# A two-layer convolution network on one core: convolution blocks of one half of the images beside the MLP of the other half, tap matrices made by TensorE, and one pool of two PSUM slots

## The chip, the cores and the metric

The kernel runs on one core of one Trainium2 chip. A core has five engines that run their own queues: TensorE (PE, matmuls, whose weight loads the profile lists as PEld), VectorE (DVE), ScalarE (ACT), GpSimd (POOL) and SyncE (SP), which only issues transfers. Sixteen DMA engines move data between the chip's main memory (DRAM) and the core's SBUF; SP, ACT and POOL each have a queue that issues them. TensorE writes to PSUM, which has eight banks of 512 fp32 values in each of 128 partitions. The metric is device microseconds (us) of one execution.

## The reference

Input x has 32 images of 96 channels and 56 x 56 positions. Everything is fp32.

```python
# layer 0
h = depthwise_conv7x7(x) + conv_b                    # 96 channels, padding 3
h = (h - mean_c(h)) * rsqrt(var_c(h) + 1e-5) * ln_g + ln_b   # over the channels
h = gelu(h @ w1 + b1) @ w2 + b2                      # 96 -> 384 -> 96, at each position
x = h * layer_scale + x
# layer 1
x = silu(depthwise_conv5x5(x) + conv_b)              # padding 2
dts, Bs, Cs = split(x_proj_w @ x)                    # 6, 4 and 4 rows
delta = softplus(dt_w @ dts + dt_b)
P = exp(cumsum(max(delta * -exp(A_logs), log 1e-9))) # along the 3136 positions
hs = P * cumsum(delta * Bs * x / max(P, 1e-9))
y = sum_n(hs * Cs) + x * Ds
```

## The kernel before, in words

The work goes in four stages, one after the other. Between them the data lies in DRAM: conv1_d after the first convolution, block_d after the MLP, conv2_d after the second convolution; each exists twice, for the two halves g of 16 images.

*Setup* (lines 94 to 274). For each convolution the taps of a channel are a small matrix that is nonzero only near a diagonal (a band), because a block puts image rows on the partitions. taps() writes the taps with zeros around them (pad) to DRAM (taps_d), and weights() reads them back many times, shifted, into wide tiles w1s (7 x 7, 6.2 MB in 16 loads) and w2s_t (5 x 5, 4.6 MB in 4), all issued by ACT. The biases come the same way (bias_d). Small constants are loaded by POOL and worked up by VectorE and a few matmuls (L218, L225).

*First convolution* (lines 313 to 382): 48 blocks, two halves g times KB = 24 groups kb of four channels. load1 has SP issue 8 loads of x into one of four tiles, three blocks ahead. bands (L300) has POOL copy the block's matrices into the order that TensorE wants (we, 3 buffers, two blocks ahead). convolve (L287) is 64 matmuls, 8 taps on 8 parts of the array. ScalarE copies the result out of PSUM (ht, L352, 3 buffers) and squares it (sq, L354, 2 buffers); POOL issues ht to conv1_d (L356); VectorE adds ht and sq to sums (acc, four additions, L365 to L368). After a half's last block, four matmuls (pm, L373) sum over the channels and a short chain over ScalarE and VectorE gives rstd_t (L378 to L382). Each block takes 4 of the 8 PSUM banks.

*MLP* (lines 385 to 499): 28 groups n of image rows, each of two units u, 56 units in all. load2 loads h (12 transfers) and x (4), three buffers each. normed scales h by rstd, which a matmul spreads over the partitions (rb, L427, then VectorE, L433). expand(u, f), for three thirds f, makes 12 matmuls into ph (L442, one buffer of 4 banks) and a Gelu on ScalarE (g, L448, 6 buffers). second(u - 1, e), for three thirds e, makes 12 matmuls into po (L464, 3 banks) and a VectorE addition of bias and x into o (L469, 2 buffers); after a group POOL issues o to block_d (L480). The order that is written out is expand(u, 0), normed(u + 1), second(u - 1, 0), expand(u, 1), second(u - 1, 1), expand(u, 2), second(u - 1, 2). So each Gelu lies beside a part of second. The profile counts each fp32 matmul as two instructions.

*Second convolution* (lines 503 to 549): as the first, with 48 matmuls a block, loads from block_d (L517), a Silu out of PSUM (st, L541, 3 buffers) and four transfers to conv2_d on POOL (L545).

*Scan* (lines 553 to 791): loads xs, projects, and runs VectorE's scans and POOL's products. The change does not touch it.

Most instructions are pinned (`pin`), which keeps them in the order of the program on their engine; a scheduler places the others. Each queue is strictly in order: an instruction that waits holds up what stands behind it.

Of the kernel before, what the change touches and what calls it, by code (L numbers as in the profile page):

```python
# [8 lines left out]
F32 = mybir.dt.float32  # L9
# [6 lines left out]
B2, BI = 2, 16  # L16
# [14 lines left out]
PARTS = (2, 4, 6, 12)  # L31
LOW = 25
S1, S2 = K1 + 1, K2 + 1
WL1, WL2 = PR * S1 + 1, PR * S2 + 1
T1, T2 = 67, 67
# [8 lines left out]
NG = 3  # L44


@with_exitstack
def convnext_then_scan_kernel(
# [27 lines left out]
    taps1_d = dram.tile([C, T1 * S1 + 1], F32, name="taps1_d")  # L76
    taps2_d = dram.tile([C, T2 * S2 + 1], F32, name="taps2_d")
    bias1_d = dram.tile([C, WL1], F32, name="bias1_d")
    bias2_d = dram.tile([C, WL2], F32, name="bias2_d")
# [8 lines left out]

    def column(src, n, name):
        t = const.tile([n, 1], F32, name=name)  # L90
        nc.gpsimd.dma_start(t, src.rearrange("(p o) -> p o", o=1))
        return t

    c1b_t = const.tile([C, 1], F32, name="c1b_t")
    c2b_t = const.tile([C, 1], F32, name="c2b_t")
    wide = ExitStack()
    wpool = wide.enter_context(tc.tile_pool(name="wide", bufs=1))
    w2s_t = wpool.tile([128, KB, 2, WL2], F32, name="w2s_t")
    mid = ExitStack()
    rstd_t = mid.enter_context(tc.tile_pool(name="mid", bufs=1)).tile(  # L100
        [128, B2, 2, TOK], F32, name="rstd_t"
    )
    first = ExitStack()
    w1pool = first.enter_context(tc.tile_pool(name="w1p", bufs=1))
    w1s = [w1pool.tile([128, n, 2, WL1], F32, name=f"w1s_{i}") for i, n in enumerate(PARTS)]
    x1s = [w1pool.tile([128, 2, COLS], F32, name=f"x1_{i}") for i in range(4)]
    for t in x1s:
        nc.vector.memset(t, 1.0)
    prep_s = ExitStack()
    prep = prep_s.enter_context(tc.tile_pool(name="prep", bufs=1))  # L110
    prep_ps = prep_s.enter_context(tc.tile_pool(name="prep_ps", bufs=1, space=PSUM))

    def weights(t, taps_d, bias_d, k, n, k0, k1, zs):
        s, wl, row = k + 1, PR * (k + 1) + 1, n * (k + 1) + 1
        for i in range(Q):
            cp, h = divmod(i, 2)
            c0 = k0 * 4 + cp
            pin(nc.scalar.dma_start(
                t[i * PR : (i + 1) * PR].rearrange("p k j w -> p (k j) w"),
                at(taps_d, c0 * row + zs[h] * s, [[s, PR], [2 * row, 2 * (k1 - k0)], [1, wl]]),  # L120
            ))
            pin(nc.scalar.dma_start(
                t[i * PR + PR - 1 : (i + 1) * PR].rearrange("p k j w -> p (k j) w"),
                at(bias_d, c0 * wl, [[wl, 1], [2 * wl, 2 * (k1 - k0)], [1, wl]]),
            ))

    def taps(taps_d, bias_d, cw, cb, cb_t, k, z, n, down):
        s = k + 1
        kt = prep.tile([C, k * k], F32, name=f"kt{k}")
        nc.scalar.dma_start(kt, cw)  # L130
        nc.scalar.dma_start(cb_t, cb.rearrange("(p o) -> p o", o=1))
        pad = prep.tile([C, n * s + 1], F32, name=f"pad{k}")
        nc.vector.memset(pad, 0.0)
        for i in range(k):
            a = k - 1 - i if down else i
            for u in range(k):
                nc.vector.tensor_copy(
                    pad[:, 1 + (z + i) * s + u : 2 + (z + i) * s + u],
                    kt[:, a * k + k - 1 - u : a * k + k - u],
                )  # L140
        nc.scalar.dma_start(taps_d, pad)
        br = prep.tile([C, PR * s + 1], F32, name=f"br{k}")
        nc.vector.memset(br, 0.0)
        nc.vector.tensor_copy(
            br[:, : PR * s].rearrange("c (m u) -> c m u", u=s)[:, :, k - k // 2],
            cb_t.to_broadcast([C, PR]),
        )
        nc.scalar.dma_start(bias_d, br)

    taps(taps1_d, bias1_d, c1w, c1b, c1b_t, K1, Z1, T1, False)  # L150
    k0 = 0
    for t, n in zip(w1s, PARTS):
        weights(t, taps1_d, bias1_d, K1, T1, k0, k0 + n, (3, 0))
        k0 += n
    taps(taps2_d, bias2_d, c2w, c2b, c2b_t, K2, Z2, T2, True)
    weights(w2s_t, taps2_d, bias2_d, K2, T2, 0, KB, (0, 3))

    ident = const.tile([128, 128], F32, name="ident")
    make_identity(nc, ident)
    eps_t = const.tile([128, 1], F32, name="eps_t")  # L160
    nc.gpsimd.memset(eps_t, LN_EPS)
    lift_t = const.tile([128, 2], F32, name="lift_t")
    nc.gpsimd.memset(lift_t[:, 0:1], LIFT)
    nc.gpsimd.memset(lift_t[:, 1:2], -LIFT)

    g_t = column(ln_g, C, "g_t")
    lnb_t = column(ln_b, C, "lnb_t")
# [3 lines left out]
    nc.gpsimd.memset(bcw_t, 0.0)  # L171
    ls_b = const.tile([128, C], F32, name="ls_b")
    nc.gpsimd.dma_start(ls_b, ls.rearrange("(o n) -> o n", o=1).to_broadcast([128, C]))
    b1_t = const.tile([128, 3], F32, name="b1_t")
    nc.gpsimd.dma_start(b1_t, b1.rearrange("(f p) -> p f", p=128))
    w2_t = const.tile([128, 3, C], F32, name="w2_t")
    nc.gpsimd.dma_start(w2_t, w2.rearrange("(f p) c -> p f c", p=128))
    dt4_t = const.tile([128, C], F32, name="dt4_t")
    nc.gpsimd.memset(dt4_t, 0.0)
    b2_t = const.tile([128, 3], F32, name="b2_t")  # L180
    ls_t = const.tile([128, 3], F32, name="ls_t")
    for q in range(Q):
        rows = slice(q * PR, (q + 1) * PR)
        nc.gpsimd.dma_start(dt4_t[q * PR : q * PR + R], dtwT)
        nc.gpsimd.dma_start(dtb_t[rows], dtb.rearrange("(g p) -> p g", p=PR))
        nc.gpsimd.dma_start(ds_t[rows], ds.rearrange("(g p) -> p g", p=PR))
        for g in range(NG):
            nc.gpsimd.dma_start(
                bcw_t[rows, g, : R + 2 * N], xpT[g * PR : (g + 1) * PR, :]
            )  # L190
        nc.gpsimd.dma_start(b2_t[rows], b2.rearrange("(g p) -> p g", p=PR))
        nc.gpsimd.dma_start(ls_t[rows], ls.rearrange("(g p) -> p g", p=PR))
    a_t = const.tile([128, NG], F32, name="a_t")
    for g in range(NG):
        nc.gpsimd.dma_start(a_t[:, g : g + 1], at(alog, g * PR, [[1, PR], [C, N], [1, 1]]))

# [8 lines left out]
    pickr_t = const.tile([128, OCT, 128], F32, name="pickr_t")  # L205

    cen = prep.tile([C, C], F32, name="cen")
    nc.vector.tensor_scalar(cen, ident[:C, :C], -1.0 / C, None, ALU.add)
    cen4 = prep.tile([C, 3, Q, PR], F32, name="cen4")
    for q in range(Q):  # L210
        nc.vector.tensor_copy(cen4[:, :, q, :], cen.rearrange("c (g p) -> c g p", g=3))
    w1_t = prep.tile([C, F], F32, name="w1_t")
    nc.gpsimd.dma_start(w1_t, w1)
    w1g = prep.tile([C, F], F32, name="w1g")
    nc.vector.tensor_scalar(w1g, w1_t, g_t, None, ALU.mult)
    for g in range(3):
        ps = prep_ps.tile([128, 512], F32, name=f"ps_w1_{g}", tag="ps_w1", bufs=2)
        nc.tensor.matmul(  # L218
            ps[:, :F], lhsT=cen4[:, g].rearrange("c q p -> c (q p)"), rhs=w1g,
            start=True, stop=True,  # L220
        )
        nc.vector.tensor_copy(w1c_t[:, g, :], ps[:, :F])
    ps = prep_ps.tile([128, 512], F32, name="ps_b1")
    for f in range(3):
        nc.tensor.matmul(  # L225
            ps[:, f : f + 1], lhsT=w1_t[:, f * 128 : (f + 1) * 128], rhs=lnb_t,
            start=True, stop=True,
        )
    nc.vector.tensor_add(b1p_t, ps[:, :3], b1_t)
    for f in range(3):  # L230
        nc.vector.tensor_mul(w2_t[:, f, :], w2_t[:, f, :], ls_b)
    nc.vector.tensor_mul(b2p_t, b2_t, ls_t)

    nc.vector.memset(pick_t, 0.0)
    for q in range(Q):
        rows = slice(q * PR, (q + 1) * PR)
        for i in range(2):
            lo = q * PR + R + i * N
            nc.vector.tensor_copy(
                pick_t[rows, i, :].rearrange("p (c n) -> p c n", n=N),  # L240
                ident[rows, lo : lo + N].rearrange("p (o n) -> p o n", o=1).to_broadcast([PR, PR, N]),
            )
        nc.vector.tensor_copy(
            pickr_t[rows].rearrange("p o (s c) -> p o s c", s=Q),
            ident[rows, q * PR : q * PR + HH]
            .rearrange("p (o s u) -> p o s u", s=Q, u=1)
            .to_broadcast([PR, OCT, Q, PR]),
        )
    nc.vector.tensor_reduce(
        sel_t, ident.rearrange("p (c n) -> p c n", n=N), axis=mybir.AxisListType.X, op=ALU.add  # L250
    )
    nc.vector.tensor_reduce(
        jsum_t[:, :64], ident.rearrange("p (j s) -> p s j", j=2),
        axis=mybir.AxisListType.X, op=ALU.add,
    )
    nc.vector.tensor_scalar(jsum_t[:, :64], jsum_t[:, :64], 1.0 / C, None, ALU.mult)
    nc.vector.tensor_copy(jsum_t[:, 64:], jsum_t[:, :64])
    for q in range(Q):
        rows = slice(q * PR, (q + 1) * PR)
# [576 lines left out]
```

## Time and profile before

| | |
|---|---|
| three runs | 3502.12, 3511.12, 3516.37 us, median 3511.12 us |
| profiled execution | 3505.03 us, span 3503.2 us |
| mean granted TensorE clock | 0.855 |
| busy | PE 2966.6, DVE 2231.7, ACT 1708.8, POOL 1967.3 us |
| copies of the first convolution (L352) | first 100.24, twelfth 195.55, 24th 286.19, 25th 303.65, last 457.55 us |
| MLP matmuls | from 487.00 us, last po near 1360 us |
| Silus of the second convolution (L541) | first 1388.94, last 1690.31 us |

Times are microseconds from the first instruction. In the slices of the page each digit is the busy share of one fortieth of the span in tenths; PEclk is the clock granted to TensorE, DMA the mean busy share of the 16 DMA engines. A line of the timeline gives start, duration, engine, line, operation, output and inputs, shapes, and in brackets the engine's idle time before it and what ended that. A line of the waits gives who waited for whom: us in total, times, longest.

### The profile page before, as it was taken

To read this page: it belongs to the slowest core of one execution; us is meant where nothing else is said; L and a number is where in the kernel's file an instruction comes from. 1 tells how busy PE (TensorE), PEld (TensorE's weight loads), DVE (VectorE), ACT (ScalarE), POOL (GpSimd) and SP (SyncE) were. 2 spreads that over 40 slices of the span, in tenths; PEclk is the share of its full clock that TensorE was granted. 3 is DMA by queue.
4 is the path that set the end of the run, shared out by engine and by line. 5 is a ranking of instruction groups with operands and counts; after the bars stand their busy time and mean duration, and the time that the engine had idled before them with its cause. 6 is when DMAs were issued, how large, how long until landed. Compare 5 with 4: busy or idle time off the path is not lost.

```text
span 3503.2 us, 65347 instructions
## 1 busy us (share of the span) xinstructions
PE 2966.6 (85%) x27660; PEld 1071.5 (31%) x27660; DVE 2231.7 (64%) x1335; ACT 1708.8 (49%) x1729; POOL 1967.3 (56%) x1096
## 2 busy tenths in 40 slices
PE   2599969999999997888688888888888888888885
PEld 1455533333333332444222222222222222222221
DVE  2498942222222221000099999999999999999998
ACT  0344433333333332222276676666667667667664
POOL 3354500000000002555388888888888988888886
PEclk9799979999999998999767787777777788777776
DMA  8898964444444434999655665646555566554652
GB/s 129 198 250 237 262 165 137 134 127 136 143 143 134 136 112 100 276 280 282 170 149 141 161 167 156 160 129 161 162 153 158 139 161 174 158 161 123 172 156 75
DMA packets 372163, 575.46 MB, mean 164 GB/s; under 512 B 217216, under 2 KB 300848, under 8 KB 371872
## 3 DMA queue, kind: packets, MB, share of 16 engines
q1 hardware_dynamic: 332352, 432.29, 45.7%
q0 software_dynamic: 25424, 127.03, 12.0%
q10 hardware_dynamic: 14096, 11.97, 2.0%
q8 instruction: 218, 3.57, 0.4%
q14 instruction: 73, 0.60, 0.1%
HBM read 366.89 MB, written 204.22 MB: 163 GB/s over the span
## 4 chain that ended last, share of the span: by engine, by line
PE 53%; ACT 16%; DMA 14%; SPq 5%; issue 4%; POOL 4%; DVE 3%; POOLq 0%; ACTq 0%; DVEq 0%
PE ph L442 12%; PE po L464 11%; PE ps L287 10%; ACT da L685 5%; PE px L611 5%; ACT da L689 4%; PE pd L680 4%; PE py L738 3%; PE py L743 3%; DMA x<-block_d 3%; DMA u<-dx_d 3%; DMA xs<-conv_d 2%; SPq L517 2%; DMA x<-in_x_dram 2%; PE pk L660 2%
## 5 line engine op out<-in xcount | busy, mean ns | idle before, releaser
L693 POOL TENSOR_TENSOR u<-u,bt 128x1568 f32<-128x1568 f32 x192 | 673.6, 3508 | 163.6 <-DMA u<-dx_d 135.5
L287 PE MATMUL ps<-x,we 32*64 32x432 f32 (+2 forms) x10752 | 602.5, 575 | 133.1 <-DMA x<-block_d 52.3
L731 POOL TENSOR_TENSOR da<-u,ct 128x1568 f32<-128x1568 f32 x192 | 673.2, 3506 | 39.7 <-DVE u L715 36.5
L448 ACT ACTIVATE g<-ph,b1p_t 128x1792 f32<-128x1792 f32 x168 | 294.9, 1755 | 561.7 <-PE ph L442 561.7
L480 POOL DMA_DIRECT2D block_d<-o x112 | 59.8, 560 | 845.2 <-DVE o L469 842.3
L287 PEld LDWEIGHTS ps<-x,we 32*64 32x64 f32 x10752 | 336.6, 136 | 399.2 <-issue 253.0
L442 PE MATMUL ph<-h,w1c_t 32*128 32x448 f32 x4032 | 432.4, 558 | 22.5 <-DVE h L433 16.2
L469 DVE SCALAR_TENSOR_TENSOR o<-po,b2p_t,x 128x448 f32<-128x448 f32 x168 | 114.9, 684 | 511.2 <-PE po L464 511.2
L464 PE MATMUL po<-g,w_t 128*32 128x448 f32 x4032 | 413.7, 543 | 2.4 <-DVE o L469 2.4
L685 ACT ACTIVATE da<-pd,lift_t,a_t 128x784 f32<-128x784 f32 x384 | 373.5, 1003 | 72.5 <-PE pd L680 60.4
L680 PE MATMUL pd<-dl,rep_t 32*128 32x392 f32 x1536 | 357.3, 607 | 49.9 <-ACT bt L664 25.5
L738 PE MATMUL py<-xs,dsm_t 32*32 32x392 f32 x1536 | 257.1, 750 | 154.6 <-ACT ct L664 101.4
L706 DVE TENSOR_TENSOR_SCAN run_t<-da,run_t 128x1568 f32<-128x1568 f32 x96 | 329.2, 3429 | 69.8 <-ACT da L689 60.2
L712 DVE SCALAR_TENSOR_TENSOR run_t<-run_t,u 128x1568 f32<-128x1568 f32 x192 | 345.6, 1800 | 20.4 <-DVE run_t L706 0.5
L706 DVE TENSOR_TENSOR_SCAN run_t<-da,cp,run_t 128x1568 f32<-128x1568 f32 x96 | 334.9, 3488 | 10.4 <-DVE u L715 0.5
L715 DVE TENSOR_TENSOR_SCAN u<-da,hp,run_t 128x1568 f32<-128x1568 f32 x96 | 334.1, 3480 | 3.4
L715 DVE TENSOR_TENSOR_SCAN u<-da,run_t 128x1568 f32<-128x1568 f32 x96 | 328.3, 3420 | 3.3
L689 ACT ACTIVATE da<-da,lift_t 128x1568 f32<-128x1568 f32 x192 | 307.8, 1603 | 5.6
L660 PE MATMUL pk<-xd,pick_t 32*128 32x392 f32 x1024 | 273.3, 723 | 15.9 <-ACT da L685 13.3
L611 PE MATMUL px<-xs,bcw_t 32*32 32x392 f32 x1536 | 234.4, 661 | 53.8 <-DMA xs<-conv_d 53.6
L442 PEld LDWEIGHTS ph<-h,w1c_t 32*128 32x128 f32 x4032 | 192.8, 187 | 263.2 <-issue 173.8
L743 PE MATMUL py<-da,sel_t 128*32 128x392 f32 x1536 | 251.4, 741 | 24.3 <-POOL da L731 24.3
(99 smaller groups left out, 2542.2 us busy)
## 6 DMA issues: line engine op xcount, KB each, us to landing
u<-dx_d SPq DMA_DIRECT2D x192, 784.0 KB, 5.1
conv_d<-ht POOLq DMA_DIRECT2D x96, 448.0 KB, 6.1
conv_d<-st POOLq DMA_DIRECT2D x192, 224.0 KB, 5.3
h<-conv_d SPq DMA_DIRECT2D x336, 112.0 KB, 2.5
x<-in_x_dram SPq DMA_DIRECT2D x112, 336.0 KB
block_d<-o POOLq DMA_DIRECT2D x112, 336.0 KB, 7.4
xs<-conv_d SPq DMA_DIRECT2D x384, 98.0 KB, 5.3
dx_d<-dx SPq DMA_DIRECT2D x256, 147.0 KB, 4.0
```

The costliest lines, as they stand in the source:

```text
L287: pin(nc.tensor.matmul(pv[:, :, lo:hi], lhsT=wt[rows, j, k - d], rhs=xv[rows, j, :, lo + e : hi + e, s], start=(t == 0), stop=(t == k), ti ...
L442: pin(nc.tensor.matmul(ph[:, q, :TOK], lhsT=w1c_t[rows, e, f * 128 : (f + 1) * 128], rhs=ht[rows, e, s], start=(e == 0), stop=(e == 2), ti ...
L464: pin(nc.tensor.matmul(po[rows, e, :TOK], lhsT=w2_t[:, f, e * PR : (e + 1) * PR], rhs=gts[u, f][:, q], start=(f == 0), stop=(f == 2), tile ...
L611: pin(nc.tensor.matmul(px[quad(j), i, :BK], lhsT=bcw_t[quad(j), g], rhs=tokens(2 * m + i, quad(j), g), start=(g == 0), stop=(g == NG - 1), ...
L680: pin(nc.tensor.matmul(ps[:, j, :BK], lhsT=rep_t[quad(q)].rearrange("p c n -> p (c n)"), rhs=dls[k][quad(q), g], start=True, stop=True, ti ...
L685: pin(nc.scalar.activation(pair(da, a), ps[:, :, :BK], AF.Relu, bias=lift_t[:, 0:1], scale=a_t[:, g : g + 1],))
L689: pin(nc.scalar.activation(da, da, AF.Exp, bias=lift_t[:, 1:2], scale=1.0))
L693: pin(nc.gpsimd.tensor_mul(us[i], us[i], bts[i // NG]))
L706: pin(nc.vector.tensor_tensor_scan(run, da[:, cut], zero, p0, ALU.mult, ALU.add))
L715: pin(nc.vector.tensor_tensor_scan(ut[:, cut], da[:, cut], run, h0, ALU.mult, ALU.add))
L731: pin(nc.gpsimd.tensor_mul(das[i], us[i], cts[i // NG]))
L738: pin(nc.tensor.matmul(py[quad(j)], lhsT=dsm_t[quad(j), g], rhs=tokens(k, quad(j), g), start=True, stop=False, tile_position=(j * PR, j * PR),
```

## The change

1. *Tap matrices.* taps, weights, taps_d and bias_d go. matrix() loads the taps of all channels to the partitions four times (once for each 32-row part of the array), makes 0/1 selection matrices (shift) from an identity, and build() multiplies the two with 8 x 16 small matmuls, whose results ScalarE and VectorE copy by turns into one wide tile w7s or w5s. The first is made at the start, the second in the middle of the MLP.
2. *PSUM.* All of the convolutions, the MLP and the builds take their PSUM from one pool of two slots of four banks. rb moves into the fourth bank of po's slot.
3. *Order.* The first half's 24 blocks of the first convolution run alone, with the setup of the small constants between them; two more blocks follow. Then the first half's 28 MLP units run with 22 blocks of the second half's first convolution between them, one at the head of each unit. The second half's 28 units run with 22 blocks of the first half's second convolution in the same way. The last 26 blocks of the second convolution run alone. Inside a unit all of second(u - 1) now stands ahead of the three expands.
4. *Buffers.* we 3 to 2, ht 3 to 2 (shared with st), sq 2 to 1, g 6 to 3, h and x 3 to 2, o 2 to 1. Both convolutions use the same four image tiles.
5. *Tables.* In the units with second-convolution blocks, one-element activations (table) ask for the Gelu and Silu tables ahead of time.

The diff, cut to its core:

```diff
+    slots = convs.enter_context(tc.tile_pool(name="slots", bufs=2, space=PSUM))
+    def slot(name):
+        return slots.tile([128, Q, 512], F32, name=name, tag="slot")
...
+    def matrix(pool, tmp, cw, cb, k, z, zs, down):
+        s = k + 1
+        kt = tmp.tile([128, C, k], F32, name=f"kt{k}")
+        tap = tmp.tile([128, C, s], F32, name=f"tap{k}")
+        pin(nc.vector.memset(kt, 0.0))
+        for q in range(Q):
+            lo = q * PR
+            pin(nc.scalar.dma_start(kt[lo : lo + k], cw.rearrange("c (i u) -> i c u", i=k)))
+            pin(nc.scalar.dma_start(
+                kt[lo + k : lo + s, :, k // 2 : k // 2 + 1],
+                cb.rearrange("(o c u) -> o c u", o=1, u=1),
+            ))
+        for v in range(1, s):
+            pin(nc.vector.tensor_copy(tap[:, :, v : v + 1], kt[:, :, k - v : k - v + 1]))
...
+        def build():
+            for a in range(PR // Q):
+                ps = slot(f"pw{k}_{a}")
+                for i in range(Q):
+                    cp, h = divmod(i, 2)
+                    for b in range(Q):
+                        base = tap[b * PR : b * PR + s, cp]
+                        pin(nc.tensor.matmul(
+                            ps[i * PR : (i + 1) * PR, b, : 2 * KB * s],
+                            lhsT=sel[b * PR : b * PR + s, h, a * Q + b],
...
+                            start=True, stop=True, tile_position=(b * PR, i * PR),
+                        ))
...
+                if a % 2:
+                    pin(nc.vector.tensor_copy(dst, src))
+                else:
+                    pin(nc.scalar.copy(dst, src))
...
+    def ahead(n, last):
+        if n + XB - 1 < last:
+            conv_load(n + XB - 1)
+        if n + WB - 1 < last:
+            bands(n + WB - 1)
+    def block1(n, last):
+        ahead(n, last)
+        ht = conv(n)
+        sq = square(n, ht)
+        return lambda: gather_sums(n, ht, sq)
...
+        for n in range(KB):
+            block1(n, half_n)()
+            if n in later:
+                later[n]()
...
+    load_h(0)
+    for n in range(KB, KB + lead):
+        sums = block1(n, half_n)
+        if n == KB:
+            norm(0)
+        sums()
...
+    normed(0, start[:, 3])
+    for u in range(2 * half_u + 1):
+        sums = None
+        if u < half_u:
+            if n1 < half_n:
+                sums = block1(n1, half_n)
+                n1 += 1
+            elif build2 is None:
+                norm(1)
...
+                build2 = matrix(w2pool, tmp, c2w, c2b, K2, Z2, (0, 3), True)
+            elif u == half_u - 4:
+                build2()
...
+        elif u >= half_u + 2:
+            if u == half_u + 2:
+                for n in range(half_n, half_n + XB - 1):
+                    conv_load(n)
...
+            if n2 < half_n + KB - 2:
+                ahead(n2, half_n + KB)
+                conv(n2)
+                table(AF.Gelu)
+                n2 += 1
+        if u or u + 1 < 2 * half_u:
+            po = slot(f"po_{u}")
+            if u + 1 < 2 * half_u:
+                normed(u + 1, po[:, 3])
+            if u:
+                second(u - 1, po)
+        if sums is not None:
+            sums()
+        if u < 2 * half_u:
             for f in range(3):
-                if u < units:
-                    expand(u, f)
-                if f == 0 and u + 1 < units:
-                    normed(u + 1)
-                if u:
-                    second(u - 1, f)
+                expand(u, f)
+            if half_u + 2 <= u + 1 and n2 < half_n + KB - 2:
+                table(AF.Silu)
+        if u % 2 and u // 2 + 2 < octs:
+            load_h(u // 2 + 2)
+        if u % 2 == 0 and u and u // 2 + 1 < octs:
+            load_x(u // 2 + 1)
+    for n in range(n2, 2 * half_n):
...
+        conv(n)
```

Here XB, WB, HB = 4, 2, 2 are the buffers of image tiles, bands and outputs; half_n = 48 is the number of blocks of one convolution and half_u = 28 that of units of one half; conv(n) is the 48 or 64 matmuls of a block with its copy out of PSUM (or Silu) and its transfers to DRAM.

## The prediction

> **What bounds the kernel now.** I read the slices of the page first, then busy time by stage, then single instructions in order of time. The slices (each 87.6 us) part the span into four stages.
>
> ```profile
> PE   2599969999999997888688888888888888888885
> DVE  2498942222222221000099999999999999999998
> PEclk9799979999999998999767787777777788777776
> DMA  8898964444444434999655665646555566554652
> ```
>
> Slices 0 to 4 are the first convolution: DMA and VectorE at 8 to 9 tenths, TensorE lower at first. Slices 5 to 15 are the middle stage (MLP): TensorE full, DMA at 4. Slices 15 to 18 are the second convolution: DMA at 9, VectorE idle. From slice 19 the scan runs, with VectorE at 9 tenths; the change leaves it alone. So what can be won lies before 1690.31 us, where the last Silu of the second convolution starts.
>
> Busy time by stage (columns: window, its length, then busy us and count of PE, weight loads, DVE, ACT, POOL, then granted clock, DMA share, GB/s):
>
> ```profile
> 176.00:263.00 87.00, 80.54 (x1573) 48.10 (x1564) 80.98 (x53) 40.82 (x25) 45.07 (x49) 0.96 0.92 249
> 345.00:395.00 50.00, 48.78 (x965) 28.43 (x957) 48.60 (x31) 24.07 (x15) 25.77 (x30) 1.00 0.93 272
> 510.00:1340.00 830.00, 830.00 (x7912) 313.79 (x7907) 201.76 (x324) 286.10 (x163) 57.71 (x108) 1.00 0.42 130
> 1500.00:1540.00 40.00, 37.01 (x608) 18.45 (x616) 0.00 (x0) 11.10 (x7) 22.87 (x36) 0.96 0.95 280
> ```
>
> The MLP has no idle TensorE at all, so work put beside it is not free: it costs its own TensorE time. What it saves is only what its block loses to DMA where it stands now. Those losses come from the starts of the copies out of PSUM: undisturbed, a first-convolution block takes 6.22 us.
>
> ```profile
> 328.57 1.66 ACT L352 COPY ht<-ps 128x1792 f32<-128x1792 f32 x1 [2.83 <-PE ps L287]
> 330.52 1.20 POOL L356 DMA_DIRECT2D conv_d<-ht  x2 [2.83 <-ACT ht L352]
> 331.72 2.21 POOL L300 COPY we<-w1s 128x512 f32<-128x512 f32 x2
> 334.79 1.66 ACT L352 COPY ht<-ps 128x1792 f32<-128x1792 f32 x1 [2.83 <-PE ps L287]
> ```
>
> From 303.65 (block 24) to 457.55 (block 47) the mean is 6.69 us. The second convolution has 6.41 us from 1388.94 to 1690.31; its 48 matmuls (96 instructions) take 4.73 us where nothing waits. Its waits name DMA on both sides:
>
> ```profile
> ACT st L541 <- DMA conv_d<-st: 95.9, 20, 7.8
> PE ps L287 <- DMA x<-block_d: 52.3, 38, 18.4
> ```
>
> One third of an MLP unit:
>
> ```profile
> 702.48 2.54 PE L442 MATMUL ph<-h,w1c_t 32*128 32x448 f32 x24
> 704.95 2.46 PE L464 MATMUL po<-g,w_t 128*32 128x448 f32 x24
> 705.15 1.76 ACT L448 ACTIVATE g<-ph,b1p_t 128x1792 f32<-128x1792 f32 x1 [3.10 <-PE ph L442]
> 707.34 2.54 PE L442 MATMUL ph<-h,w1c_t 32*128 32x448 f32 x24
> ```
>
> 4.86 us a third; with the rb matmul (0.74) a unit is 15.32 us, and 56 units are 858 us. The bigger reserve is at the seams, where TensorE stands:
>
> ```profile
> 487.00 4.34 PE L442 MATMUL ph<-h,w1c_t 32*128 32x448 f32 x24 [16.20 <-DVE h L433]
> 1378.07 14.76 PE L287 MATMUL ps<-x,we 32*64 32x448 f32 x204 [18.36 <-DMA x<-block_d]
> ```
>
> From the last copy of the first convolution (457.55) to steady MLP (511.45) 54 us pass for one unit's ph; the other seam costs 18.4 us and a cold first block (Silu at 1388.94, 10.9 us after the matmuls began). And the start: block 0 is copied at 100.24 and block 11 only at 195.55, while 11 MB of tap matrices come through DRAM.
>
> **The change, step by step.** Times are when TensorE gets there.
>
> (a) Setup, to the first convolution matmul: 52 us. The DRAM tap matrices go; the taps are read in four copies of 7 x 96 runs of 28 B, 2688 packets. Their tile is cleared after the four image tiles (before: pad at 8.42 us), so they start at 9. No row has such packets. Low: q1's 332352 packets took 45.7% of 16 engines, 77 ns each, so 13 us. High: a load of xs has 448 packets and lands in 5.3 us; six such in a row are 32 us. I take 13, because the 16 engines carry little else then but images. Then some 5 us of small VectorE copies; eight rounds of 16 small matmuls, each emptied by ScalarE or VectorE. A round: 32 instructions at the convolution's 49 ns are 1.6 us, double when cold, and an eviction of 1536 elements is 1.4 us by L352's 1653 ns for 1792. Two slots hide part: 2.5 us a round, between 1.6 and 4.6, 20 us in all. Then bands, 2.2. Sum 49; VectorE's setup copies, put in front and waiting for POOL's 41 small loads (0.55 us each), make it 52. Ends: 43 and 85.
>
> The Trainium skill, in DMA: Bandwidth & Descriptors (section Why a DMA increments its semaphore by 16 and not by 1), speaks against this step: a DMA uses the largest number of engines up to 16 that divides its slowest dimension, which for 7 rows is 7. By that, 2688 x 77 ns on 7 engines would be an estimated 30 us, and the sum 17 us more; no row of the trace shows such a load.
>
> (b) 24 blocks at 6.69, a cold start of 3 (at 1380 to 1385 eight matmuls took 0.75 us, later 0.39) and setup_mlp's matmuls (4.2 + 1.4): to 221. Before, block 23 was copied at 286.19. With two buffers of bands, POOL must copy out and issue (1.95 + 1.20) and make bands (2.2 to 3.1) while one block runs: 5.4 to 6.3 against 6.22, just hidden; if not, see rival 1.
>
> (c) Blocks 24, 25, 26 with norm between: three blocks 18.7, pm 5.8 (L373). rstd is ready 10.9 us after pm (before: 297.1 to 308.0), so the first rb stands 5; then VectorE has two sums (6 us each) ahead of the scaling and ph stands 6 more; pm waits 2. With 1.5 of switches 39: to 260, against 54 plus 11 (the norm between 286.19 and 303.65) before.
>
> (d) Rest of unit 0: 7. (e) Units 1 to 21: conv 6.22 + 15.0 + 0.1 each, 447: to 715. The 15.0 lies between 14.6 (three ph, three po, rb and fewer switches between them) and 15.32. The order of slots is pc, po, ph, ph, ph in turn over two slots: a ph slot is wanted again 2.25 us after its end, its Gelu is done after 1.76 + 0.15; po's VectorE evictions (0.14 + 0.69) end inside the next ph. VectorE has 6.4 of sums (means 1.16, 2.79, 1.30, 1.15) and 3.9 of MLP work in 21.3 us; DMA moves 1.8 + 2.0 MB, 180 GB/s where 270 were seen.
>
> (f) Unit 22: pm 5.8, then the second tap matrix's VectorE work is queued in front of unit 22's scaling and po evictions, waiting for taps in 1920 packets (9 to 23 us by (a)'s two rows) that ScalarE issues only after its Sqrt (5 us). 5 + 9 + 5 of copies + 3.7 against 9.8 of TensorE's own work: 13 to 27 of standing, I take 15; the unit is 35. Units 23 to 29 are 105, the build 15 (12 to 25): to 870.
>
> (g) The first loads of block_d stand on SP behind load_h(16): 12 issues 8.4 us, 8 issues 6, landing 5, so TensorE stands 18 and starts cold, 3: to 891.
>
> (h) 22 units with a second-convolution block: 4.73 + 15.0 + 0.1, 436: to 1327. Two table loads of 1.28 us a unit lie beside po and the next block; their cover gone, they cost 56 us. (i) Four units and the last po: 67, to 1394. (j) Two blocks lie inside the wait for block_d, as long as the old seam: 18.4, to 1412. (k) A cold block 10.9 and 23 at 6.7 (6.41, and 0.3 for two output buffers): to 1577.
>
> (l) For 43 mixed units I add 0.5 us each for waits at slot switches that no row shows (0 to 2): 21. Last Silu at 1598 against 1690.31: 92 us less. The profiled execution took 3505.03 (span 3503.2 and 1.8 around it), so 3413; the median of the runs, 3511.12, lies 6 above it, inside the range. Of the 92, some 65 come from the start and some 47 by overlap (22 x 0.47 + 22 x 1.68); the seams and shorter units give the rest, and (f), (g) and (l) take back.
>
> **Rivals.**
> 1. *Shallow buffers bind.* Output buffers go from 3 to 2, sq to 1, bands to 2. For: ScalarE already waited 95.9 us with three; st issued by 1503.66 was down at 1516.4, 12.7 us later. With two that is (4 + 12.7)/2 = 8.35 us a block, 38 us more in (k); and if POOL's 6.3 plus switches makes 7.5, 19 more in (b): 3470. Against: such landing is the backlog that a third buffer allows; the bytes are the same.
> 2. *Tap loads are slow.* Both at their high end: 19 in (a) and 12 in (f), and the build cold and serial, 10: 3454. For: nothing moves beside them. Against: images load meanwhile.
> 3. *Slots serialize (slower).* If the turn of the two slots puts two of three Gelus in TensorE's way, as at 494.62 to 506.56 where one ph followed another only after 5.8 to 6.1 us, each costs 1.76 + 0.34. Two in 56 units are 235 us on a sum without (l) of 3392: 3627. It decides from 2.4 us a unit on. Against: the turn above leaves 0.3 us of slack at each.
> 4. *The overlap is none*: a block beside the MLP costs as much as alone, because TensorE is full. Then (e) and (h) lose 47: 3460; with rival 1 as well 3517, no change. For: TensorE at 830 of 830 us. Against: the undisturbed 6.22 and 4.73 us are rows of the trace.
>
> **Numbers.** Forecast (3360 to 3445) 0.55; rival 1 0.18; rival 2 0.10; rival 4 alone 0.05; rivals 1 and 4 together (3490 to 3520) 0.07; rival 3 0.05. Faster by over 0.5%, which is about what a measurement can tell from no change: 0.88; within 0.07; slower 0.05. The range, 3360 to 3480, leaves out rival 3, rivals 1 and 4 together, and the ends of the others.
>
> **What would show it.** First convolution matmul near 52, block 23's copy near 221; mixed units of 21.3 and 19.8 us with granted clock 1.00 and no PE idle over 1 us in them; one gap of 15 after the second pm and one of 18 before the first block_d block; the last Silu near 1600; the scan as long as before (1813 us). Wrong would be: ph or pc waiting for ACT g in every unit, convolution blocks over 7.5 us, POOL bands as the releaser of ps.

## The result, and the profile after

The changed kernel takes 3647.54 us (median of four runs, 3643.86 to 3653.64) against 3511.81 for the kernel before: **3.9% slower**, ratio 1.0392 [1.0365, 1.0419]. Forecast was 3413, faster. The profiled execution has a span of 3642.1 us. Its last Silu stands at 1825.05 us, the scan takes 1817 us from there (before: 1813): nearly the whole miss, 227 us against the forecast 1598, lies ahead of the scan.

The slices of the changed kernel (each 91 us), as those of before:

```profile
PE   5988888886878888888968888888888888888885
DVE  5973333333111111110029999999999999999998
PEclk9999999997989999999967777777787777777776
DMA  5995555532355655527855546656655655655652
```

The DMA work is spread as the change meant it: 5 in most slices between the first blocks and the last, where before it stood at 8 or 9 beside the convolutions and at 4 beside the MLP; VectorE is at 3 beside the first convolution's blocks and at 1 beside the second's. But TensorE, which stood at 9 through the whole MLP before, is at 8 in nearly every slice. So time is lost in every unit, not at one place. By stage (a stretch of mixed units with first-convolution blocks, then one with second-convolution blocks; columns as before: window, length, busy us and count of PE, weight loads, DVE, ACT, POOL, then granted clock, DMA share, GB/s):

```profile
323.10:771.70 448.60, 391.06 (x4659) 171.51 (x4659) 154.04 (x170) 146.50 (x85) 74.51 (x100) 0.95 0.51 142
1070.80:1523.90 453.10, 388.64 (x4598) 169.61 (x4598) 70.99 (x114) 188.06 (x152) 91.35 (x150) 0.99 0.55 159
```

TensorE is idle for 58 of 449 us and for 64 of 453 us, with DMA at half and VectorE at about a third or less: nothing is full. What it waits for, from the waits up to 1850 us (us in total, times, longest; pc is the PSUM tile of a convolution block):

```profile
PE po L510 <- DVE h L483: 118.6, 54, 24.2
PE po L510 <- DVE o L515: 90.3, 112, 0.8
PE pc L313 <- DMA xc<-block_d: 22.3, 12, 12.0
PE ph L491 <- ACT g L497: 1.0, 1, 1.0
```

Two of these lines carry the result: 209 us in which po waits for VectorE, 54 times for the scaling of h (L483; 24.2 of it is one stall at a seam) and 112 times, twice a unit, for the eviction of o (L515). One unit shows how (timeline; TensorE, then VectorE beside it):

```profile
480.54 1.01 PE L477 MATMUL po<-rstd_t,pickr_t 32*128 32x448 f32 x2
483.33 3.63 PE L510 MATMUL po<-g,w_t 128*32 128x448 f32 x24 [1.77 <-DVE h L483]
487.75 4.20 PE L510 MATMUL po<-g,w_t 128*32 128x448 f32 x24 [0.79 <-DVE o L515]
492.77 2.46 PE L510 MATMUL po<-g,w_t 128*32 128x448 f32 x24 [0.82 <-DVE o L515]
495.16 7.05 PE L491 MATMUL ph<-h,w1c_t 32*128 32x448 f32 x72
502.14 6.55 PE L313 MATMUL pc<-xc,we 32*64 32x448 f32 x128
```
```profile
481.59 1.68 DVE L483 TENSOR_TENSOR h<-h,po 128x448 f32<-128x448 f32 x3 [7.01 <-PE po L477]
487.01 0.69 DVE L515 SCALAR_TENSOR_TENSOR o<-po,b2p_t,x 128x448 f32<-128x448 f32 x1 [3.73 <-PE po L510]
492.03 0.69 DVE L515 SCALAR_TENSOR_TENSOR o<-po,b2p_t,x 128x448 f32<-128x448 f32 x1 [4.33 <-PE po L510]
```

rb is written into po's fourth bank, VectorE reads it from there for 1.68 us, and only then may the first third of po begin, though it writes another bank. Between the thirds the same: each waits until VectorE has read the third before it. TensorE stands 1.77 + 0.79 + 0.82 = 3.4 us a unit, and two of the groups in this unit run at 3.63 and 4.20 us in place of 2.46.

### The profile page after: what moved, and what is told of

Read it like the earlier page. It is cut to its first block, busy times and chain, and to the rows that moved or that the text cites. A ratio compares the mean times of both kernels' runs of the same rounds, so it can differ in the third digit from the quotient of the medians.

```text
span 3642.1 us, 66140 instructions
## 1 busy us (share of the span) xinstructions
PE 3021.4 (83%) x28172; PEld 1132.9 (31%) x28172; DVE 2220.9 (61%) x1317; ACT 1787.3 (49%) x1827; POOL 1963.1 (54%) x1092
## 4 chain that ended last, share of the span: by engine, by line
PE 50%; ACT 16%; DMA 13%; DVE 9%; SPq 6%; POOL 3%; issue 3%; POOLq 0%; ACTq 0%; DVEq 0%
PE po L510 13%; PE pc L313 9%; PE ph L491 8%; ACT da L768 5%; PE px L694 5%; ACT da L772 4%; PE pd L763 4%; PE py L821 3%; PE py L826 3%; DMA xs<-conv_d 3%; DVE o L515 2%; DVE h L483 2%; DMA xc<-block_d 2%; ACT dl L720 2%; SPq L675 2%
## 5 line engine op out<-in xcount | busy, mean ns | idle before, releaser
L510 PE MATMUL po<-g,w_t 128*32 128x448 f32 x4032 | 464.6, 598 | 209.5 <-DVE h L483 118.6
L313 PE MATMUL pc<-xc,we 32*64 32x432 f32 (+2 forms) x10752 | 596.7, 564 | 36.1 <-DMA xc<-block_d 22.3
L313 PEld LDWEIGHTS pc<-xc,we 32*64 32x64 f32 x10752 | 379.4, 133 | 247.5 <-issue 130.2
L515 DVE SCALAR_TENSOR_TENSOR o<-po,b2p_t,x 128x448 f32<-128x448 f32 x168 | 115.0, 684 | 498.0 <-PE po L510 498.0
L483 DVE TENSOR_TENSOR h<-h,po 128x448 f32<-128x448 f32 x165 | 92.6, 617 | 528.9 <-PE po L477 412.3
L491 PE MATMUL ph<-h,w1c_t 32*128 32x448 f32 x4032 | 395.4, 540 | 2.0 <-ACT g L497 1.0
L388 POOL DMA_DIRECT2D conv_d<-ht x192 | 101.4, 536 | 424.8 <-ACT ht L384 409.9
L378 POOL DMA_DIRECT2D conv_d<-ht x96 | 57.6, 605 | 437.5 <-ACT ht L376 434.7
L510 PEld LDWEIGHTS po<-g,w_t 128*32 128x32 f32 x4032 | 121.9, 116 | 548.3 <-DVE o L515 195.7
```

The source lines that it names most:

```text
L313: pin(nc.tensor.matmul(pv[:, :, lo:hi], lhsT=wt[rows, j, k - d], rhs=xv[rows, j, :, lo + e : hi + e, s], start=(t == 0), stop=(t == k), ti ...
L491: pin(nc.tensor.matmul(ph[:, q, :TOK], lhsT=w1c_t[quarter(q), e, f * 128 : (f + 1) * 128], rhs=ht[quarter(q), e, s], start=(e == 0), stop= ...
L510: pin(nc.tensor.matmul(po[quarter(q), e, :TOK], lhsT=w2_t[:, f, e * PR : (e + 1) * PR], rhs=gts[u, f][:, q], start=(f == 0), stop=(f == 2) ...
```

## The experiments

Theory T: the loss is TensorE waiting for VectorE's reads of the tile that it writes next, because rb lies in po's tile and po's thirds follow one another directly; to it T adds the time that matmuls lose at a lower granted clock beside these waits. Rival R1: mixing itself makes the units long (DMA contention, clock). Rival R2: the loss lies at the seams between the stages.

| run | edit, in a few words | us | ratio to before |
|---|---|---|---|
| e1_rb_last | after: rb and scaling behind po | 3541.31 | 1.0088 [1.0064, 1.0112] |
| e2_evict_last | after: three thirds, then three evictions | 3540.09 | 1.0079 [1.0053, 1.0104] |
| e3_reads_last | after: all of VectorE's reads behind all of po | 3456.36 | 0.9845 [0.9822, 0.9868] |
| e4_po_then_conv | e3, and the block behind po | 3390.80 | 0.9660 [0.9632, 0.9687] |
| e5_seams | after: only the seams | 3616.23 | 1.0270 [1.0239, 1.0302] |
| e6_both | e4 and e5 | 3374.82 | 0.9591 [0.9571, 0.9612] |
| e7_no_mix | e6 without blocks beside units | 3477.52 | 0.9894 [0.9862, 0.9926] |
| e8_late_taps | e6, tap loads behind the Gelus | 3359.72 | 0.9562 [0.9547, 0.9576] |
| b1_rb_in_po | before: rb in po's tile | 3616.31 | 1.0276 [1.0254, 1.0299] |
| b2_thirds_one_tile | before: thirds in a row | 3904.00 | 1.1115 [1.1092, 1.1138] |
| b3_thirds_three_tiles | b2, one tile a bank | 3853.27 | 1.0964 [1.0946, 1.0982] |

The kernel before was measured again beside each group of runs: 3510.61 us (e1 to e4), 3518.52 (b1, e5 to e7) and 3513.61 (b2, b3, e8). A difference of times from two groups is uncertain by about as much as these differ.

**One wait at a time.** e1_rb_last moves the rb matmul and the scaling behind po and its evictions:

```diff
-            if u + 1 < 2 * half_u:
-                normed(u + 1, po[:, 3])
             if u:
                 second(u - 1, po)
+            if u + 1 < 2 * half_u:
+                normed(u + 1, po[:, 3])
```

> Edit: only the place of the rb matmul and the scaling of h that reads it: behind the three thirds of po and their evictions, not ahead of them. Theory T (TensorE's po matmuls wait for VectorE's readers of the same tile): the wait of 1.77 us ahead of the first third goes, in 55 units, but the two waits of 0.8 us between the thirds stay, and ph may now wait for the scaling at the unit's end (0.3 to 1.0 us). Net 63 to 110 us less: 3535 to 3585. Rival R1 (mixing itself, DMA contention and clock, makes the units long): under 15 us either way, 3630 to 3660. Rival R2 (the loss lies at the seams between stages): 3630 to 3660 as well.

e2_evict_last leaves rb in front and takes the evictions out of the loop over the thirds:

```diff
                         tile_position=(0, q * PR),
                     ))
+        for e in range(3):
             pin(nc.vector.scalar_tensor_tensor(
```

> Edit: the three thirds of po's matmuls run in a row, and the three evictions follow; rb and the scaling stay ahead of them. Theory T: the two waits of 0.8 us between the thirds go in 56 units (about 90 us), the 1.77 us ahead of the first stays; ph1 may wait for the last eviction, under 1 us; the granted clock of the mixed units of the first half, 0.93, rises and gives up to 50 more. 3500 to 3570. R1 and R2: 3630 to 3660.

They gained 106 and 107 us, inside T's ranges; R1 and R2 had expected 3630 us or more. How the gain divides was not foreseen. In e1 a new wait took part of the old one's place (rb now waits 0.81 us for the last eviction, 47 times), so that the waits for VectorE at po fell from 209 to 152 us; about as much again, 56 us, is TensorE's busy time ahead of the scan (1534 to 1478 us for the same matmuls). In e2 the waits fell to 120 us and the busy time by some 25. The granted clock of the mixed units, 0.95 and 0.99 in the changed kernel (first and second half of the images), is 1.00 and 1.00 in e1 and 0.97 and 0.95 in e2: higher in the first half, lower in the second.

**Both waits.** e3_reads_last splits normed into the matmul and scaled(), and lets second call scaled between its 36 matmuls and its three evictions. e4_po_then_conv puts the convolution block between po and the expands, in place of ahead of po:

```diff
+        if u or u + 1 < 2 * half_u:
+            po = slot(f"po_{u}")
+            ...
+                second(u - 1, po, scale)
+            ...
         if u < half_u:
             if n1 < half_n:
-                sums = block1(n1, half_n)
+                ahead(n1, half_n)
+                late = (n1, conv(n1))
+                sums = lambda: gather_sums(*late, square(*late))
```

> Edit: rb and all 36 x 3 matmuls of po first, then all of VectorE's reads of that tile (scaling, three evictions). No wait stands inside po any more; what may take its place is ph waiting for the scaling of h where no convolution block stands between (units without a block), and ph1 for the evictions (1.6 us). Theory T: 1.77 + 2 x 0.8 = 3.4 us less in each of 55 units is 187, and 20 to 80 of it come back as the wait ahead of ph1: 3475 to 3540. R1 and R2: 3620 to 3660.

> Edit: as the kernel with the reads last, and in each mixed unit rb and po stand ahead of the convolution block, so that the block's matmuls (4.7 to 6.2 us) lie over VectorE's reads of po's tile. Theory T: nearly all 187 us of waits go in the mixed units (43), and the clock of the first half's units returns to 0.98 or more (another 20 to 40): 3400 to 3460. R1: the units of 26.4 and 23.7 us stay over 24 and 22: 3580 or more. R2: 3620 to 3660.

e3 is 191 us below the changed kernel, e4 257 us. Both come out somewhat below T's ranges, because matmuls that run faster gave more than T had put down: in e3 the waits for VectorE at po and ph are still 67 us, and TensorE's busy time ahead of the scan is 63 us less; in e4 they are 11 us and 86. In e3 po runs in one piece and the wait has become a smaller one in the middle of ph (timeline of e3_reads_last):

```profile
451.17 6.97 PE L513 MATMUL po<-g,w_t 128*32 128x448 f32 x72
458.08 2.54 PE L494 MATMUL ph<-h,w1c_t 32*128 32x448 f32 x24
461.82 4.79 PE L494 MATMUL ph<-h,w1c_t 32*128 32x448 f32 x48 [1.21 <-DVE o L520]
```

ph's second third wants po's slot, which VectorE is still reading. In e4 the block stands over those reads, and a unit with a first-convolution block has no gap at all, one with a second-convolution block 0.3 us (a unit's timeline, and its windows of the same two stretches of blocks):

```profile
424.21 7.09 PE L494 MATMUL ph<-h,w1c_t 32*128 32x448 f32 x72
431.12 0.91 PE L477 MATMUL po<-rstd_t,pickr_t 32*128 32x448 f32 x2
431.96 6.97 PE L513 MATMUL po<-g,w_t 128*32 128x448 f32 x72
438.87 6.48 PE L313 MATMUL pc<-xc,we 32*64 32x448 f32 x128
```
```profile
319.20:677.10 357.90, 357.90 (x4662) 149.21 (x4663) 152.07 (x170) 144.45 (x86) 74.79 (x103) 1.00 0.64 180
908.30:1290.40 382.10, 376.89 (x4602) 155.28 (x4603) 65.78 (x114) 183.92 (x153) 90.12 (x151) 1.00 0.69 193
```

Seventeen units in 357.9 us are 21.05 us each, nineteen in 382.1 are 20.1: the forecast's 21.3 and 19.8, with the same work, the same transfers and the same buffers. R1 has fallen.

**The other direction.** b1_rb_in_po takes the kernel before and only puts rb in a fourth bank of po's tile:

```diff
-            rb = ps_h.tile([128, 512], F32, name=f"rb_{u}", tag="rb")
+            po = ps_h.tile([128, Q, 512], F32, name=f"po_{u}", tag="po")
+            ots[u - 2, "ps"] = po
+            rb = po[:, 3]
```

> Edit of the kernel before, nothing else of the change: rb is put into the fourth bank of po's tile in place of a tile of its own. Theory T: po's first third now waits for the scaling of h that reads rb, some 2 us in each of 56 units at most: 3560 to 3640. R1 (contention and clock from mixing): no change, 3500 to 3520. A value between, 3520 to 3560, would say that the wait is real but that the order of before, with ph between the thirds of po, covers most of it.

It costs 98 us (3616.31 against 3518.52), and one line of its waits up to 1850 us, with one line of its timeline, accounts for it:

```profile
PE po L467 <- DVE h L435: 95.8, 54, 1.8
```
```profile
808.73 2.46 PE L467 MATMUL po<-g,w_t 128*32 128x448 f32 x24 [1.77 <-DVE h L435]
```

rb takes a whole bank in both kernels; only the tile that it belongs to differs.

**Tile or bank?** b2_thirds_one_tile puts the thirds of po in a row in the kernel before. b3_thirds_three_tiles does the same with three tiles of one bank:

```diff
-                ots[u, "ps"] = ps_h.tile([128, 3, 512], F32, name=f"po_{u}", tag="po")
+                ots[u, "ps"] = [
+                    ps_h.tile([128, 1, 512], F32, name=f"po_{u}_{b}", tag=f"po{b}")
+                    for b in range(3)
+                ]
```

> Edit of the kernel before: the three thirds of po stand in a row behind the first third of ph, as in the changed kernel; po stays one tile of three banks, rb a tile of its own. Theory T: two waits of 0.8 us a unit appear between the thirds (56 x 1.62 = 91 us), beside what ph now waits for its Gelu (ph has one buffer: two turns of 2.1 us a unit, 235 us): 3790 to 3860. Compared only with the next run, which has the same order.

> Edit: as the run with the thirds in a row, but po is three tiles of one bank each in place of one tile of three banks; the same matmuls in the same order and in as many banks. If the wait belongs to the tile (the program lets a writer of one bank wait for a reader of another bank of the same tile): the two waits between the thirds go, 70 to 100 us less than the run with one tile. If it belongs to the memory (any reader holds up any writer) or to what the eviction itself takes: no difference.

The timelines of one unit, first with one tile, then with three (there with the first eviction, on VectorE):

```profile
934.90 2.46 PE L464 MATMUL po<-g,w_t 128*32 128x448 f32 x24
938.17 2.46 PE L464 MATMUL po<-g,w_t 128*32 128x448 f32 x24 [0.81 <-DVE o L469]
941.44 2.46 PE L464 MATMUL po<-g,w_t 128*32 128x448 f32 x24 [0.81 <-DVE o L469]
```
```profile
930.94 6.97 PE L467 MATMUL po<-g,w_t 128*32 128x448 f32 x72
933.47 0.68 DVE L472 SCALAR_TENSOR_TENSOR o<-po,b2p_t,x 128x448 f32<-128x448 f32 x1 [0.74 <-PE po L467]
```

With three tiles the two waits are gone, and the eviction runs beside matmuls into the next bank. So the wait goes with the tile, not with the memory: the program makes a writer of one bank wait for a reader of another when both belong to one tile. The Trainium skill, in Perfetto Trace Analysis (section Optimizing Tensor Performance, Matmuls), advises rotating independent groups through banks so that the emptying of one overlaps the matmuls of the next; b3 agrees, and b2 shows that separate banks are not enough while one tile holds them. The gain was 51 us, not the 70 to 100 expected: from 510 to 1300 us the granted clock is 0.95 in b2 and 0.87 in b3, and TensorE's busy time ahead of the scan is 49 us longer in b3 (1626 against 1577): slower matmuls took back some half of the 90.6 us that the two waits are in b2. Two expectations missed by this: the size of the gain, and b2 itself, which took 3904.0 us where 3790 to 3860 was expected; its waits came as expected (90.6 us between the thirds, 217.0 for Gelus, where 91 and 235 were), but its TensorE is busy 93 us longer ahead of the scan than in the kernel before (1577 against 1484).

**The seams.** e5_seams puts VectorE's part of the second tap matrix from the head of unit 22 to the end of unit 23, when its taps have landed (one unit later, not the seven of the expectation), and issues the first loads of block_d ahead of load_h(16):

```diff
-                build2 = matrix(w2pool, tmp, c2w, c2b, K2, Z2, (0, 3), True)
+                build2 = matrix(w2pool, tmp, c2w, c2b, K2, Z2, (0, 3), True, split=True)
...
+        if u == half_u - 5:
+            build2 = build2()
+        if u == half_u + 1:
+            for n in range(half_n, half_n + XB - 1):
+                conv_load(n)
```

(The bands of those blocks move along.)

> Edit of the changed kernel at its two seams alone: VectorE's part of the second tap matrix is put seven units later, when its taps have landed, and the first loads of block_d are issued ahead of the last loads of h. Theory T: the standing of 24 us in unit 22 and some 12 to 18 us ahead of the first block of the second convolution go, no more: 3600 to 3625. R2 (the seams are the loss): under 3560. R1: 3600 to 3625 as theory T.

It gained 31 us (43 by the ratios to the kernel before): R2 has fallen, though the standing was real (the 24 us became 10.75, and the 12 ahead of the first block of the second convolution went). e6_both joins it to e4:

> Edit: reads last, po ahead of the block, and both seams mended together. Theory T: the two gains add up, about 36 us below the kernel with po ahead of the block alone: 3370 to 3430, faster than the kernel before (3511) and the changed one. R1: 3550 or more.

Here the seams gave only 16 us on top (24 by the ratios to the kernel before). In e4's order TensorE stands 13.22 us at the first seam, for a Gelu, and the seams' edit leaves that wait as it is; what went is 6.87 us of standing for POOL's bands at the second seam, with the slow block behind it (8.59 us, then 5.01). What was left at the first seam is the first line below, of e6_both's timeline: the Gelu stands on ScalarE behind the issues of the tap loads. In e8_late_taps matrix() is called behind the expands of unit 22, and the second line is its answer:

```profile
741.29 4.51 PE L497 MATMUL ph<-h,w1c_t 32*128 32x448 f32 x24 [13.80 <-ACT g L503]
```
```profile
732.54 2.54 PE L497 MATMUL ph<-h,w1c_t 32*128 32x448 f32 x24 [1.72 <-ACT g L503]
```

> Edit of the kernel with both mended: ScalarE issues the loads of the second tap matrix behind the three Gelus of unit 22, not ahead of them. In the mended kernel's trace TensorE stands 13.8 us there for a Gelu that stands behind those issues. Theory T and the reading of that line: 10 to 14 us less than the mended kernel, 3360 to 3366. If the wait only moves to the Gelus of unit 23: no change, 3371 to 3379.

It took 15 us more (10 by the ratios; expected were 10 to 14). At 3359.72 us, 4.4% below the kernel before, it is the best version; the slices of its profiled execution have TensorE at 9 again:

```profile
PE   5989999999999999886888888888888888888885
PEclk9999999999999999997777778787777788787776
```

**What mixing is worth.** e7_no_mix keeps everything of e6 but runs the blocks by themselves.

> Edit: the kernel with both mended, but no convolution block beside a unit: all 24 blocks of the second half of the images run ahead of the MLP, and the second convolution behind it. This prices the mixing alone. The prediction's steps (e) and (h): 21 x 0.47 and 22 x 1.68 us, 47 in favour of mixing, so about 47 above the mixed one. R1 or the prediction's rival 4: no difference or the mixed one slower.

It costs 103 us, twice what was expected. Its units last 16.08 us (from 1015.22 to 1031.30 between two po), 1.21 us of which is the wait of ph for VectorE that e4's block covers: 43 units x 1.21 = 52 us. The rest is the block's own: 7.13 us alone (20 blocks from 257.8 to 400.4) and 6.57 (47 from 1347.2 to 1656.1), where the mixed unit adds 21.05 - 14.87 = 6.18 and 20.1 - 14.87 = 5.23, so 21 x 0.95 + 22 x 1.34 = 49 us. The prediction's 47 for the overlap was right as a sum, in part by luck: its terms, 10 for the first convolution's blocks and 37 for the second's, came out at 20 and 29. That a block also covers waits was not in it.

## Why the prediction was wrong, point by point

All times are of the profiled execution of the changed kernel.

- **(a), (b) right.** First convolution matmul 53.33 (52), block 23 copied at 222.6 (221). The tap copies on VectorE begin at 23.36 (22), though, right behind an instruction that had waited for a small load of POOL's (6.36 us, ds_t), so the taps may have been there sooner: 3164 packets of ScalarE's queue took 3.0% of 16 engines in the first 60 us, 9 ns each, where (a) had counted 77. By the seven engines of the Trainium skill's rule (DMA: Bandwidth & Descriptors, section Why a DMA increments its semaphore by 16 and not by 1), cited in (a), 2688 x 9 ns would be an estimated 3.5 us; no row shows how many engines there were. The sum of (a) fits in part by luck: the eight rounds took 23.6 us (20), 7.22 of them a wait of TensorE for a copy of VectorE's that itself stood behind two more waits for ds_t (3.88 and 4.75).
- **(c), (d) right** with 4 us to spare: unit 1 begins at 262.9 (267). The first rb stood 4.66 us (5), but ph only 0.96 (6).
- **(e) wrong: this is the step that failed.** 21 units took 556 us, 26.5 each, not 21.3: 108 us over. The "15.0" was put between two sums of matmul times, with a reserve of 0.5 a unit in (l) for waits "that no row shows". A row of before did show them; the prediction had read the middle of the MLP, where ph stands between the thirds, and not its end, where the last po has no ph beside it:

```profile
1350.72 2.46 PE L464 MATMUL po<-g,w_t 128*32 128x448 f32 x24 [0.81 <-DVE o L469]
1353.98 2.46 PE L464 MATMUL po<-g,w_t 128*32 128x448 f32 x24 [0.81 <-DVE o L469]
```

  The step said "po's VectorE evictions (0.14 + 0.69) end inside the next ph": true of the last third alone. And rb was costed as a matmul; that its reader now holds po was not seen. Of the 5.4 us by which a unit of 26.5 exceeds e4's 21.05, 3.4 are the waits and 2.0 matmuls that run slower (17 units: 391.06 us busy against 357.90).
- **(h) wrong, (i) and (f)'s plain units too, by the same step.** The 22 units took 23.8 us each (19.8), 88 us over, with the cold first block counted under (g); units 23 to 29 144 us (105); the four units and the last po 84.6 (67). Together with (e) 253 us, more than the whole miss.
- **(f), the stall:** 24.24 us in the first po of unit 22, forecast 15; the unit 49.7, forecast 35, inside the bounds of 13 to 27 for the standing. The parts show in the trace: the reciprocal (5.75) ahead of the clearing of kt on VectorE, 8.10 of waiting for the taps, 5 of copies. The build took 11.3 (15).
- **(g), (j), (k) right in size:** 12.0 of waiting and a cold block of 10.94, some 18 together (21); 15.1 (18.4); 159 us (165). In (j) the reason differs: the standing inside it, 5.15 us, ended with POOL's bands, not with a load of block_d.
- **(l)** reserved 21 us for slot switches. In e4 none is needed; its mixed units stand within 0.3 us of (e) and (h).
- **Rival 1** (shallow buffers) falls: from 1678.04 to 1825.05 us 23 blocks take 6.39 us each with two output buffers. **Rival 2** falls with (a) and with the build of 11.3 in (f). **Rival 3** gave 3627, near the result, for another reason: it had TensorE waiting for Gelus, and the line `ph <- ACT g` is 1.0 us in all. **Rival 4** falls with e7. The chance for slower, 0.05, belonged to a mechanism that did not occur; the one that did was on no list.

So the plan of the change and the sizes of most of its parts were sound. The order inside a unit, of VectorE's reads of po's tile and of the convolution block, cost 257 us, and mending it turns 3.9% slower into 3.4% faster (e4).

## What to carry to other kernels

When a small PSUM result moves into a tile that a longer chain writes, or when matmul groups of one tile come to stand side by side, list who reads that tile and what stands between the reads on TensorE: each reader becomes a wait (here 1.77 and 0.81 us) unless other work covers it. Put the reads behind all writes of the tile and independent matmuls over the reads, or give each bank its own tile. Read the first and last pieces of a loop in the old trace: there its cover is missing, and the wait that a new order will expose stands in plain sight.

## What the runs showed of the hardware that was not expected

The granted clock was lower in units with short waits, and how much lower did not follow the sum of the waits. The mixed units of the changed kernel with first-convolution blocks, 3.4 us idle of 26.5 and never over 1.8 at once, run at 0.95, in a stretch of 10 us around one of the waits at 0.83, in the next at 1.00:

```profile
375.00:385.00 10.00, 7.43 (x54) 1.84 (x50) 2.37 (x4) 3.35 (x2) 3.40 (x4) 0.83 0.48 106
385.00:395.00 10.00, 9.19 (x99) 4.26 (x96) 5.55 (x6) 3.51 (x2) 0.00 (x0) 1.00 0.01 2
```

e1, with three waits of 0.8 us a unit, runs at 1.00 and b1, with one of 1.77, at 0.99; e2, with one of 1.77 as well, at 0.97 and 0.95; b3, with less idle time than b2, falls from 0.95 to 0.87. The Trainium skill, in TensorE: Matmul & The Clock Gate (section A second HAM failure mode: psum-queue depth-cycling), describes such an alternation from small idle times between groups, for bf16 matmuls; the two stretches, 0.83 and then 1.00, are of that kind. What decides in which pattern it happens stays open: no run varied the waits alone.
